# Gathers by row list in a sparse two-layer graph kernel: indices clamped in the list step, no bound on the gathers

## The chip, the cores and the metric

The kernel runs on one core of one Trainium2 chip. The metric is the device time of one execution in microseconds (us); the number given for the kernel before is the median of three runs. Beside these runs, one execution was recorded by the hardware profiler, and every duration of a single instruction below comes from that record.

## The reference

The inputs are 3327 nodes with 512 features each (`x`), and one weighted adjacency matrix `adj` (3327 x 3327, float32). An edge exists with a probability that falls with both node numbers, so the first nodes (hubs) have many neighbours and the last ones few; every node has an edge to itself. Two layers follow each other; each normalizes first and adds its result to `x`:

```python
# layer 0
h = relu(layernorm(x))
x = x + adj @ (relu(adj @ (h @ W1) + b1) @ W2) + b2
# layer 1
h = relu(layernorm(x))
ts = adj @ h
attn_a = sigmoid(concat([ts, h]) @ Wa.T + ba)      # attn_b: same with Wb, bb
g = h @ W_sa
scores = (g @ a_left)[:, None] + (g @ a_right)[None, :]
e = where(adj != 0, exp(-leaky_relu(scores, 0.01)), 0)
x_a = (e / (sum(e, axis=1) + 1e-5)) @ g
x_b = adj @ (h @ W_gcnb) + b_gcnb
x = x + sigmoid(attn_a * x_a + attn_b * x_b)
```

Layer 0 is done with dense products over the whole matrix. Layer 1 needs, for a group of nodes, only the rows of `h` for which the matrix isn't zero, and the kernel uses that.

## The kernel before

The nodes are padded to 3328 (`NP`), 26 blocks (`NB`) of 128. The matrix comes in transposed and padded with zeros (`adjT`), so row 3327, the last one, holds only zeros. A row of `adjT` is also seen as 104 groups (`NG`) of 32 floats (`GW`), 128 bytes each: `adj_groups` lists them all, row by row.

**Pass 1** makes the first product of layer 0. It goes over 7 chunks of 512 columns (the last has 256) and in each over 26 row blocks `j`. SyncE loads a 128 x 512 tile `a` of the matrix into one of 8 buffers; TensorE adds it to `acc_u` (line 512); VectorE takes the largest absolute value of every group of 32 columns into `most` (line 516). Both readers have to be done before the buffer is loaded again.

From `most` the generator `make_lists` makes, a chunk later, the lists for layer 1: for each block of 128 nodes, which is 4 groups of 32, the numbers of the rows that have a nonzero in the group. It is moved forward one step behind each `most` of the next chunk, so its small VectorE operations (`at` L446, `past` L463, `jb` L468 and L469, then `row_h` L473 and `row_a` L476) and its small matmuls (`p_list` L457) lie among the large ones. A batch handles up to 18 list columns of 128 places; 16 batches make 228 columns (`NL`). `rooms` says how many places per group a block has: 9, 8, 7, 6 and 6 for blocks 1 to 5, then 5, 4 and in the end 3, each times 64. Block 0, the hubs, is treated densely (`acc_hub`, line 644).

The number of a list place is computed in float32 in `jb`. A place that no row fills, an empty place, gets a number of at least 3328. Two int32 lists are written from `jb`: `row_h`, the row number with 3327 as its maximum, and `row_a`, row number times 104 plus the group's number, the index of a 128-byte group.

**Pass 2** makes the second product of layer 0 (`acc_g`, line 685) with the matrix loaded again, then the new rows `x` and `h`. The rows of `h`, 520 floats long with a node's score in column 512, are stored to `h_rows` in memory.

**Gathers.** Both lists are used by one helper, `gather` (line 139), which issues an indirect DMA from GpSimd (POOL) for one list column: 128 indices, one row for each partition. 228 of them fetch adjacency groups into `ae` during passes 1 and 2. They are issued in the order of `gather_adj`, each behind one matmul of line 512 or 685 (`gather_behind`, which skips every third or fifth). The `ae` tiles are set to zero at the start (line 379). The other 228 fetch rows of `h` in stage 3 into a cycle of 16 pairs of buffers, shown as `rows` and `hr`.

**Stage 3** is layer 1, block by block from 25 down to 1. `attend` issues a block's row gathers, adds the scores (L800), takes the exponential and masks it by the gathered adjacency (`masked_exp`, L206 to L208); `sums` multiplies weights by rows (`acc`, L829); `turn` transposes (`ptt`, L843), `weigh` multiplies by `W_gcnb` and `W_sa` (`p_b` L883, `p_a` L890), `finish` writes the result. The order in which the engines get this is written out by hand with `queued` (after these instructions), and `pace` holds the gathers of a block behind the sums of the block three or four before (`LEAD`).

A gather here carries the bound that the change is about: with `bounds_check=last, oob_is_err=False` an index above `last` is skipped, and the destination keeps what it held. The bound is an operand in a register. In `row_a` the empty places exceed it; in `row_h` none do.

Of the kernel before, what the change touches and what calls it, by code (L numbers as in the profile page):

```python
# [11 lines left out]
ALU = mybir.AluOpType  # L12
# [34 lines left out]
def kernel(  # L47
# [17 lines left out]
    nc = tc.nc  # L65
    NP, D = x.shape
# [5 lines left out]
    NG = NP // GW  # L72
# [39 lines left out]
    h_dram = dram.tile([NP, ROW], F32, tag="h_rows", name="h_rows")  # L112

    row_h = kept([P, NL], "row_h", I32)
    row_a = kept([P, NL], "row_a", I32)
# [5 lines left out]
    def segments(i):  # L121
# [9 lines left out]
    rows = [  # L131
        hubp.tile([P, 2, ROW], F32, tag=f"rows{k}", name=f"rows{k}", bufs=1) for k in range(NR // 2)
    ]
# [1 line left out]
    for t in rows:  # L135
        nc.vector.memset(t[:, :, D:], 0.0)

    def gather(dst, table, rows, last):
        return nc.gpsimd.indirect_dma_start(  # L139
            out=dst, out_offset=None, in_=table,  # L140
            in_offset=bass.IndirectOffsetOnAxis(ap=rows, axis=0),
            bounds_check=last, oob_is_err=False,
        )

    adj_groups = adjT.rearrange("j (b i) -> (j b) i", i=GW)
# [2 lines left out]
    def gather_adj():  # L148

        for i in range(1, NB):  # L150
            r = rooms[i]
            for k0, k1 in segments(i):
                for q in range(2):
                    for k in range(k0, k1):
                        while (i, q) not in listed:
                            yield None
                        f = first[i] + q * r + k
                        yield gather(
                            ae[i][:, 2 * k0 + q * (k1 - k0) + k - k0, :GW], adj_groups,
                            row_a[:, f : f + 1], NP * NG - 1,  # L160
                        )

    columns = gather_adj()
# [52 lines left out]
    with (  # L216
# [165 lines left out]
        def make_lists(c, most):  # L382


            c0, w = chunks[c]
            g0, n = c0 // GW, w // GW

            def small(shape, name, dtype, bufs=2):
                return l0w.tile(shape, dtype, tag=name, name=f"{name}_{c}", bufs=bufs)

            flag = small([P, MG, NB], "flag", BF16)
            nc.vector.tensor_scalar(flag[:, :n, :], most[:, :n, :], 0.0, None, op0=ALU.is_gt)

            upto = small([P, MG, NB], "upto", BF16)
            flat = "p b j -> p (b j)"
            nc.vector.tensor_tensor_scan(
                upto[:, :n, :].rearrange(flat), begin[:, :n, :].rearrange(flat),
                flag[:, :n, :].rearrange(flat), 0.0, op0=ALU.mult, op1=ALU.add,
            )
            count = small([P, MG], "count", BF16)  # L400
            nc.vector.tensor_copy(count[:, :n], upto[:, :n, NB - 1])
            after = small([P, MG, NB], "after", BF16)
            nc.vector.tensor_tensor(
                after[:, :n, :], count[:, :n].unsqueeze(2).to_broadcast([P, n, NB]),
                upto[:, :n, :], ALU.subtract,
            )
            yield
            p_off = bank(psB, f"p_off_{c}")
            nc.tensor.matmul(p_off[:, :n], before, count[:, :n], start=True, stop=True)
            nc.tensor.matmul(p_off[:, MG : MG + n], every, count[:, :n], start=True, stop=True)  # L410
            offset = small([P, MG], "offset", F32)
            nc.vector.tensor_copy(offset[:, :n], p_off[:, :n])
            nc.vector.tensor_tensor(
                size[:, g0 : g0 + n], p_off[:, MG : MG + n], limit[:, g0 : g0 + n], ALU.is_gt
            )


            step = steps[c % 2]
            p_sh = bank(psB, f"p_sh_{c}")
            nc.tensor.matmul(  # L420
                p_sh[:, : n * NB], shift, after[:, :n, :].rearrange(flat), start=True, stop=True
            )
            nc.vector.tensor_tensor(
                step[:, :n, :NB], p_sh[:, : n * NB].rearrange("p (b j) -> p b j", j=NB),
                upto[:, :n, :], ALU.add,
            )
            yield
            batches = []
            for i in range(c0 // P, (c0 + w) // P):
                for q in range(2 if rooms[i] else 0):  # L430
                    if not batches or sum(rooms[k] for k, _ in batches[-1]) + rooms[i] > CW // NT:
                        batches.append([])
                    batches[-1].append((i, q))
            for batch in batches:
                col = {}
                m = 0
                for i, q in batch:
                    col[i, q] = m
                    m += rooms[i]
                f0 = first[batch[0][0]] + batch[0][1] * rooms[batch[0][0]]  # L440
                at = l0w.tile([P, CW // NT, 2, HALF], BF16, tag="at", name=f"at_{f0}")
                for i, q in batch:
                    r, k = rooms[i], col[i, q]
                    for h in range(2):
                        b = NQ * i + 2 * h + q - g0
                        nc.vector.tensor_scalar(  # L446
                            at[:, k : k + r, h, :],
                            place_row[:, : r * HALF].rearrange("p (k m) -> p k m", m=HALF),
                            offset[:, b : b + 1], None, op0=ALU.is_ge,
                        )  # L450
                    yield
                pl = bank(psB, f"p_list_{f0}")
                plv = pl[:, : m * NT].rearrange("p (c j) -> p c j", j=NT)
                for i, q in batch:
                    for k in range(col[i, q], col[i, q] + rooms[i]):
                        for h in range(2):
                            nc.tensor.matmul(  # L457
                                plv[h * HALF : (h + 1) * HALF, k, :], at[:, k, h, :],
                                step[:, NQ * i + 2 * h + q - g0, :], start=True, stop=True,
                            )  # L460
                yield
                past = l0w.tile([P, CW // NT, NB], BF16, tag="past", name=f"past_{f0}", bufs=1)
                nc.vector.tensor_tensor(  # L463
                    past[:, :m, :], plv[:, :, :NB],
                    place_col[:, f0 : f0 + m].unsqueeze(2).to_broadcast([P, m, NB]), ALU.is_le,
                )
                jb = l0w.tile([P, CW // NT], F32, tag="jb", name=f"jb_{f0}")
                nc.vector.tensor_reduce(jb[:, :m], past[:, :m, :], axis=AX.X, op=ALU.add)  # L468
                nc.vector.scalar_tensor_tensor(  # L469
                    jb[:, :m], jb[:, :m], float(P), plv[:, :, NB], op0=ALU.mult, op1=ALU.add  # L470
                )

                nc.vector.tensor_scalar(  # L473
                    row_h[:, f0 : f0 + m], jb[:, :m], float(NP - 1), None, op0=ALU.min
                )
                nc.vector.scalar_tensor_tensor(  # L476
                    row_a[:, f0 : f0 + m], jb[:, :m], float(NG), group_col[:, f0 : f0 + m],
                    op0=ALU.mult, op1=ALU.add,
                )
                listed.update(batch)  # L480
                yield
# [285 lines left out]
    with tc.tile_pool(name="spw", bufs=2) as spw:  # L767
# [8 lines left out]
        def attend(i, seg):  # L776
# [11 lines left out]
            hr = taken[i][k0] = []  # L788
            for k in range(n):
                hr.append(next(pairs))  # L790
                for q in range(2):
                    f = first[i] + q * r + k0 + k
                    with queued(gathered[0]):
                        gathered[0] = gather(
                            hr[k][:, q, :], h_dram[:, :], row_h[:, f : f + 1], NP - 1
                        )
                    lead = LEAD[i < NB - 8]
                    if k0 + k + q == 0 and len(combined) >= lead:
                        pace(gathered[0], combined[-lead])
                nc.vector.tensor_tensor(  # L800
                    e.rearrange("p (q k) i -> p k q i", q=2)[:, k],
                    s_l, hr[k][:, :, D : D + 1].to_broadcast([P, 2, GW]), ALU.add,
                )
# [3 lines left out]
            if k0:  # L807
                part = spw.tile([P, 2, GW], F32, tag="part", name=f"part_{i}_{k0}")
            last = nc.vector.tensor_reduce(
                part, e.rearrange("p (q k) i -> p q i k", q=2), axis=AX.X, op=ALU.add  # L810
            )
            if k0:
                last = nc.vector.tensor_tensor(es, es, part, ALU.add)
# [121 lines left out]
        ty, last = copy_out(NB - 1, taken[NB - 1]["acc"])  # L935
        turning = NB - 1, ty, taken[NB - 1]["es"]
        held = [copied, last]
        for i in range(NB - 2, 1, -1):
# [18 lines left out]
            ty, last = copy_out(i, taken[i]["acc"])  # L957
# [159 lines left out]
```

## Time and profile before

| | |
|---|---|
| median of three runs | 844.46 us (844.13 to 846.61) |
| span of the profiled execution (first to last instruction) | 840.2 us |
| median less span | 4.3 us |
| TensorE busy | 781.6 us, 93% of the span |
| VectorE busy | 515.6 us, 61% |
| GpSimd busy | 493.4 us, 59% |
| mean granted TensorE clock | 0.973 of full speed |
| bytes moved by DMA | 200.14 MB |
| list step (first `jb` to last `row_a`) | 73.3 to 245.6 us |
| adjacency gathers | 76.3 to 423.5 us |
| row gathers | 444.8 to 792.0 us |

For the profiled execution only the span is recorded; its own total isn't listed, so the median stands beside it. The busy share of an engine is a mean over stages that differ: pass 1 ends near 210 us, pass 2 near 440 us, and stage 3 takes the rest. In the rows that follow, the number after the bar is the busy time of a group, then the mean ns of one instruction, and after the second bar the idle time just before them with what ended most of it. "issue" means that the engine waited for nothing that the profile shows.

### The profile page before, as it was taken

To read this page: it belongs to the slowest core of one execution; us is meant where nothing else is said; L and a number is where in the kernel's file an instruction comes from. 1 tells how busy PE (TensorE), PEld (TensorE's weight loads), DVE (VectorE), ACT (ScalarE), POOL (GpSimd) and SP (SyncE) were. 2 spreads that over 40 slices of the span, in tenths; PEclk is the share of its full clock that TensorE was granted. 3 is DMA by queue.
4 is the path that set the end of the run, shared out by engine and by line. 5 is a ranking of instruction groups with operands and counts; after the bars stand their busy time and mean duration, and the time that the engine had idled before them with its cause. 6 is when DMAs were issued, how large, how long until landed. Compare 5 with 4: busy or idle time off the path is not lost.

```text
span 840.2 us, 12143 instructions
## 1 busy us (share of the span) xinstructions
PE 781.6 (93%) x3615; PEld 416.9 (50%) x3615; DVE 515.6 (61%) x1658; ACT 187.6 (22%) x396; POOL 493.4 (59%) x513
## 2 busy tenths in 40 slices
PE   9999899999799999999999599799998999999795
PEld 7774344445443444444464366455554555454363
DVE  7778989999646866685775455345535353443342
ACT  7770000000002313033052022122222222121121
POOL 3202756676677777776716555666766767667400
PEclk9999999999799999999999799899999999999798
DMA  8787998898578989998958556787788867777600
GB/s 272 242 292 227 330 283 262 285 299 276 151 236 297 368 281 306 319 343 284 345 180 260 158 182 196 216 227 217 225 225 215 228 203 227 207 210 209 187 26 30
DMA packets 106891, 200.14 MB, mean 238 GB/s; under 512 B 16801, under 2 KB 30656, under 8 KB 106816
## 3 DMA queue, kind: packets, MB, share of 16 engines
q1 hardware_dynamic: 72592, 124.40, 45.2%
q0 software_dynamic: 25536, 63.74, 27.9%
q10 hardware_dynamic: 8688, 11.15, 3.8%
q8 instruction: 30, 0.49, 0.2%
q14 instruction: 45, 0.37, 0.1%
HBM read 179.39 MB, written 20.55 MB: 238 GB/s over the span
## 4 chain that ended last, share of the span: by engine, by line
PE 66%; issue 18%; DMA 7%; DVE 5%; another core or an unknown queue 3%; ACT 1%; SPq 0%; ACTq 0%; DVEq 0%
PE acc L829 14%; PE p_b L883 12%; PE p_a L890 11%; PE acc_g L685 10%; PE acc_u L512 5%; PE acc_hub L644 3%; DMA a<-in_adjT_dram 3%; PE ptt L843 3%; PE pu L291 3%; PE px L587 2%; DMA W_sa_sb<-in_W_sa_dram 1%; PE pt L283 1%; DMA xb<-in_x_dram 1%; DVE junk L563 1%
## 5 line engine op out<-in xcount | busy, mean ns | idle before, releaser
L139 POOL DMA_INDIRECT ae<-in_adjT_dram,row_a x228 | 246.4, 1081 | 151.6 <-issue 57.8
L139 POOL DMA_INDIRECT hr<-h_rows,row_h x140 | 144.1, 1029 | 64.5 <-issue 30.8
L685 PE MATMUL acc_g<-a,g 128*128 128x512 f32 (+1 forms) x364 | 160.3, 575 | 5.7 <-DMA a<-in_adjT_dram 3.8
L512 PE MATMUL acc_u<-a,rows 128*128 128x512 f32 (+1 forms) x364 | 159.9, 578 | 2.8 <-DMA a<-in_adjT_dram 2.2
L139 POOL DMA_INDIRECT rows<-h_rows,row_h x88 | 90.7, 1031 | 69.2 <-DVE e_hub L206 20.3
L883 PE MATMUL p_b<-W_g_sb,tyT 128*128 128x257 f32 x416 | 102.0, 395 | 16.3 <-issue 15.7
L516 DVE TENSOR_REDUCE most<-a 128x16 f32<-128x512 f32 (+1 forms) x182 | 110.6, 638 | 6.1 <-DMA a<-in_adjT_dram 5.2
L685 PEld LDWEIGHTS acc_g<-a,g 128*128 128x128 f32 x364 | 67.0, 192 | 85.5 <-issue 61.1
L883 PEld LDWEIGHTS p_b<-W_g_sb,tyT 128*128 128x128 f32 x416 | 78.3, 193 | 48.5 <-issue 19.3
L890 PE MATMUL p_a<-W_sa_sb,tyT 128*128 128x512 f32 (+2 forms) x216 | 97.5, 590 | 3.5 <-issue 3.1
L512 PEld LDWEIGHTS acc_u<-a,rows 128*128 128x128 f32 x364 | 66.5, 194 | 58.7 <-issue 51.9
L829 PE MATMUL acc<-hr,ae 64*64 64x512 f32 x560 | 81.7, 612 | 3.2 <-issue 2.3
L858 DVE COPY tyT<-ptt 128x512 f32<-128x512 f32 x51 | 34.9, 686 | 54.2 <-PE acc L829 21.8
L890 PEld LDWEIGHTS p_a<-W_sa_sb,tyT 128*128 128x128 f32 x216 | 41.1, 193 | 47.1 <-issue 45.6
L208 DVE SCALAR_TENSOR_TENSOR ae<-ae 128x192 f32<-128x192 f32 (+2 forms) x36 | 12.5, 368 | 79.1 <-issue 29.9
L829 PE MATMUL acc<-rows,ae 64*64 64x512 f32 x352 | 49.0, 607 | 1.7 <-issue 1.4
L829 PEld LDWEIGHTS acc<-hr,ae 64*64 64x64 f32 x560 | 30.9, 137 | 39.2 <-issue 37.9
L748 ACT ACTIVATE f<-f 128x2 f32<-128x2 f32 x26 | 5.3, 203 | 166.9 <-DVE f L747 118.4
L300 ACT ACTIVATE gT<-acc_u,b_col 128x512 f32<-128x512 f32 (+1 forms) x7 | 4.6, 657 | 157.1 <-issue 101.3
L563 DVE SCALAR_TENSOR_TENSOR junk<-rows,w_rows 128x512 bf16<-128x512 f32 x52 | 35.7, 686 | 3.0 <-issue 0.5
L716 DVE TENSOR_TENSOR xb<-xb,b_row 128x512 f32<-128x512 f32 x26 | 17.7, 689 | 30.4 <-DMA xb<-in_x_dram 19.6
L843 PEld LDWEIGHTS ptt<-ident,ty 128*128 128x128 f32 x208 | 24.5, 144 | 19.1 <-issue 18.2
(142 smaller groups left out, 907.5 us busy)
## 6 DMA issues: line engine op xcount, KB each, us to landing
a<-in_adjT_dram SPq DMA_DIRECT2D x338, 256.0 KB
h_rows<-rows SPq DMA_DIRECT2D x26, 260.0 KB
x<-in_x_dram SPq DMA_DIRECT2D x26, 256.0 KB
xb<-in_x_dram SPq DMA_DIRECT2D x26, 256.0 KB
x<-xb ACTq DMA_DIRECT2D x26, 256.0 KB
x1b<-x SPq DMA_DIRECT2D x26, 256.0 KB
out_dram<-va SPq DMA_DIRECT2D x25, 256.0 KB
ae<-in_adjT_dram,row_a POOLq DMA_INDIRECT x228
```

The lines of the kernel that those rows point to most:

```text
L139: return nc.gpsimd.indirect_dma_start(out=dst, out_offset=None, in_=table, in_offset=bass.IndirectOffsetOnAxis(ap=rows, axis=0), bounds_ch ...
L291: nc.tensor.matmul(pu[:, :HID], hT[:, k, :], W1_sb[:, k, :], start=(k == 0), stop=(k == KD - 1))
L512: added = nc.tensor.matmul(acc[:, :w], u[j], a[:, :w], start=(j == 0), stop=(j == NB - 1))
L516: nc.vector.tensor_reduce(most[:, : w // GW, j], a[:, :w].rearrange("p (b i) -> p b i", i=GW), axis=AX.X, op=ALU.max, apply_absolute_value ...
L563: return nc.vector.scalar_tensor_tensor(junk, h, 1.0, w_rows[:, s, :], op0=ALU.mult, op1=ALU.mult, accum_out=into)
L644: nc.tensor.matmul(acc_hub[k], s, hrow[i % NR][:, :D], start=(i == 0), stop=(i == NB - 1))
L685: added = nc.tensor.matmul(acc[:, :w], g[j], a[:, j % per, :], start=(j == 0), stop=(j == NB - 1))
L829: added = nc.tensor.matmul(taken[i]["acc"][h][q * HALF : (q + 1) * HALF, :], both[half_p, q * n + k, :], taken[i][k0][k][half_p, q, :D], s ...
L843: moved = nc.tensor.transpose(pt[:, k * P : (k + 1) * P], ty[h][:, k * P : (k + 1) * P], ident)
L858: last = nc.vector.tensor_copy(dst, src)
L883: nc.tensor.matmul(p_b[n][:, :WH], tyT[:, k, 0, :], W_g_sb[:, k, n * WH : (n + 1) * WH], start=(k == 0), stop=(k == KD - 1),)
L890: last = nc.tensor.matmul(p_a[:, c0:c1], tyT[:, k, 1, :], W_sa_sb[:, k, c0:c1], start=(k == 0), stop=(k == KD - 1),)
```

## The change

The helper no longer sets a bound. In the list step the minimum of `jb` and 3327 is written back into `jb`, a copy converts it into `row_h`, and `row_a` is computed from the clamped `jb`. The real list places get the same indices as before. An empty place now has the index of its group in the last row, and its gather fetches 128 bytes of zeros where before it was skipped.

```diff
-    def gather(dst, table, rows, last):
+    def gather(dst, table, rows):
         return nc.gpsimd.indirect_dma_start(
             out=dst, out_offset=None, in_=table,
             in_offset=bass.IndirectOffsetOnAxis(ap=rows, axis=0),
-            bounds_check=last, oob_is_err=False,
         )
...
                         yield gather(
                             ae[i][:, 2 * k0 + q * (k1 - k0) + k - k0, :GW], adj_groups,
-                            row_a[:, f : f + 1], NP * NG - 1,
+                            row_a[:, f : f + 1],
                         )
...
-                nc.vector.tensor_scalar(
-                    row_h[:, f0 : f0 + m], jb[:, :m], float(NP - 1), None, op0=ALU.min
-                )
+                nc.vector.tensor_scalar(jb[:, :m], jb[:, :m], float(NP - 1), None, op0=ALU.min)
+                nc.vector.tensor_copy(row_h[:, f0 : f0 + m], jb[:, :m])
                 nc.vector.scalar_tensor_tensor(
                     row_a[:, f0 : f0 + m], jb[:, :m], float(NG), group_col[:, f0 : f0 + m],
                     op0=ALU.mult, op1=ALU.add,
                 )
...
                         gathered[0] = gather(
-                            hr[k][:, q, :], h_dram[:, :], row_h[:, f : f + 1], NP - 1
+                            hr[k][:, q, :], h_dram[:, :], row_h[:, f : f + 1]
                         )
```

In the built program 456 register moves on POOL, one ahead of each gather, are gone; VectorE has 16 more operations, one copy for each batch. The order of POOL's and ScalarE's instructions is the same. On TensorE some 27 instructions around `acc_u`, `p_list` and the turns of pass 1 stand a few places earlier or later, and so do some of `at` and `most` on VectorE.

## The prediction

> **What bounds the kernel now.** I begin with the page's first part, busy time by engine, and its fifth, the costliest groups, of which I take the three gather rows.
>
> ```profile
> PE 781.6 (93%) x3615; PEld 416.9 (50%) x3615; DVE 515.6 (61%) x1658; ACT 187.6 (22%) x396; POOL 493.4 (59%) x513
> ...
> q0 software_dynamic: 25536, 63.74, 27.9%
> ...
> L139 POOL DMA_INDIRECT ae<-in_adjT_dram,row_a x228 | 246.4, 1081 | 151.6 <-issue 57.8
> L139 POOL DMA_INDIRECT hr<-h_rows,row_h x140 | 144.1, 1029 | 64.5 <-issue 30.8
> ...
> L139 POOL DMA_INDIRECT rows<-h_rows,row_h x88 | 90.7, 1031 | 69.2 <-DVE e_hub L206 20.3
> ```
>
> TensorE is 93% busy, so over the whole kernel nothing else can gain much. GpSimd is 59% busy, nearly all of it 228 + 228 gathers. The gathers' own queue (q0) takes 27.9% of the DMA engines' time. The shares differ by stage, so I read one window in pass 1, one in pass 2, one in stage 3. Columns: window, us, then busy us of PE, PEld, DVE, ACT, POOL, then PE clock, DMA share, GB/s.
>
> ```profile
> 100.00:200.00 100.00, 95.56 (x480) 43.45 (x478) 94.13 (x242) 2.06 (x3) 63.74 (x63) 0.98 0.90 285
> 300.00:400.00 100.00, 97.26 (x232) 41.79 (x230) 66.63 (x222) 26.40 (x50) 74.21 (x66) 1.00 0.93 310
> 600.00:700.00 100.00, 95.67 (x530) 53.31 (x530) 45.66 (x165) 22.22 (x49) 70.98 (x69) 1.00 0.79 222
> ```
>
> In pass 1 two engines are full, TensorE and VectorE (94%), and the DMA share is 0.90; in pass 2 TensorE and the DMA (0.93); in stage 3 TensorE alone. VectorE in pass 1 is where the new copy goes, the DMA in passes 1 and 2 is where the padded fetches go. Next, who waits in 80 to 210 us (total us, times, longest):
>
> ```profile
> PE acc_u L512 <- DMA a<-in_adjT_dram: 2.2, 1, 2.2
> PE p_list L457 <- DVE at L446: 1.0, 2, 0.5
> PE p_list L457 <- DVE row_a L476: 0.9, 1, 0.9
> ...
> DVE past L463 <- PE acc_u L512: 5.5, 6, 2.5
> DVE most L516 <- DMA a<-in_adjT_dram: 1.5, 2, 0.9
> ```
>
> In 130 us TensorE waits 1.9 us for VectorE (L457, twice for `at`, once for `row_a`), and VectorE 5.5 us for TensorE: they run in step, VectorE slightly ahead. SyncE's loads of adjacency tiles wait 25.9 us there for `acc_u` and 11.3 us for `most` to free a buffer, so VectorE also meters the transfers.
>
> **What the Trainium skill says.** "DMA: Bandwidth & Descriptors", section "SWDGE vs HWDGE vs iDMA": descriptors of a GpSimd DMA are computed in software on the GpSimd's cores. The trace agrees in so far as a gather occupies POOL for 1.00 us whether its rows have 128 or 2080 bytes. The same page, "Issuing engines are not separate DMA queues": DMAs of all issuers share 16 engines and interleave. So extra gather bytes compete with the tiles that SyncE loads; q0 and q1 are each spread over the 16 in the packet records. "VectorE: DVE Perf Modes", section "TRN2 errata — SBUF-src ops pay a fixed extra latency per instruction": a measured fixed term of about 150 cycles at 0.96 GHz, 156 ns. The trace agrees: 160 to 168 ns for the 16-column operations below. No page prices a bound on the indices.
>
> **The change, part by part.** First the bound. The built program loses 456 register moves on POOL, one per gather; its order and waits are otherwise as before.
>
> ```profile
> L139 POOLq MOVE  x456: 29/29/29, 24.0 to 790.4; - x152
> ...
> L139 POOL DMA_INDIRECT ae<-in_adjT_dram,row_a x228: 991/997/2724, 76.3 to 423.5; - x114
> L139 POOL DMA_INDIRECT hr<-h_rows,row_h x140: 992/998/1328, 450.1 to 772.3; - x140
> ```
>
> 456 × 29 ns = 13.2 us of POOL's sequencer. It is work in the 0.30 us between gathers: the timeline has them at 444.77, 446.15, 447.45, 448.75, 450.06, a period of 1.30 us. Where that shows:
>
> ```profile
> 444.77 1.08 POOL L139 DMA_INDIRECT rows<-h_rows,row_h  x1 [20.29 <-DVE e_hub L206]
> ...
> 456.11 0.22 DVE L800 TENSOR_TENSOR ae<-s_left,hr 128x64 f32<-128x64 f32 x1 [1.12 <-DMA hr<-h_rows,row_h]
> ...
> 457.92 1.19 PE L829 MATMUL acc<-rows,ae 64*64 64x512 f32 x8 [0.80 <-issue]
> ```
>
> In passes 1 and 2 POOL waits for the pace (22.5 us for `acc_u`, 11.9 for `acc_g`) and has 20.29 us between its last adjacency gather and the first row gather, so there the saving is hidden. At the start of stage 3 the six gathers of block 25 and their landings lead to the first scores at 456.11 and the first sum at 457.92, before which TensorE idles 0.80 us. Six moves are 6 × 29 = 0.17 us; I take −0.3, since the instruction may also shorten a little, with at most −0.8 (the whole idle time). Late next is the 9.4 us for which TensorE idles from 461.85 (`p_b` L883, "issue"), which may swallow it. Later in stage 3 a block of 3 places takes POOL 6 × 1.30 = 7.8 us of a block's 10.8 us, of 4 places 10.4 of 12.4, of 5 places 13.0 of 14.7; gathers land two to three blocks ahead of use. Those moves hide behind TensorE's sums and weights, and cost nothing if that cover goes, since they are only removed.
>
> What the trace doesn't show is a gather without a bound. In the one direction: the 1.00 us holds for gathers with no empty place and with 60% of them, so the test of an index costs nothing that depends on its outcome; a compare less per descriptor is worth at most a tenth of the instruction (my guess), −0.1 us each. In the other: if descriptors come from another routine, it could be slower; the slack above is the protection. I take 0, and keep ±0.1 us in the range, which gives −0.6 to +0.6 us at the start of stage 3 and nothing beyond, unless the coupling of rival D is real.
>
> Second, the copy. Before, each of 16 batches ended in these three:
>
> ```profile
> L469 DVE SCALAR_TENSOR_TENSOR jb<-jb,p_list x16: 145/160/166, 74.4 to 245.3; 128x16 f32<-128x16 f32 x5, 128x18 f32<-128x18 f32 x3, 128x14 f32<-128x14 f32 x2, 128x15 f32<-128x15 f32 x2
> L473 DVE TENSOR_SCALAR row_h<-jb x16: 155/166/361, 75.1 to 245.5; 128x16 int32<-128x16 f32 x5, 128x18 int32<-128x18 f32 x3, 128x14 int32<-128x14 f32 x2, 128x15 int32<-128x15 f32 x2
> L476 DVE SCALAR_TENSOR_TENSOR row_a<-jb,group_col x16: 154/168/293, 75.2 to 245.6; 128x16 int32<-128x16 f32 x5, 128x18 int32<-128x18 f32 x3, 128x14 int32<-128x14 f32 x2, 128x15 int32<-128x15 f32 x2
> ```
>
> Now the minimum goes back into `jb` and a copy follows it: 16 × 0.16 = 2.6 us more on VectorE. Behind it on VectorE are `row_a` and the next reductions `most`; for `row_a` wait the batch's gathers (hidden: nothing reads them before stage 3), for `most` the next loads, and for `at` the `p_list` matmuls. Both ends: 0, if VectorE's 5.5 us of waits for TensorE absorb it; +2.6, if all of it pushes through `most` to the tiles. The waits say VectorE is mostly ahead, the 94% says not by much. I choose a third, +0.9. The scheduler also moves some 27 matmuls of `acc_u` and `p_list` by a few places; nothing is added there, ±0.4.
>
> Third, the padded places. Of 29,184 list places 5,888 (20.2%) are empty; in the packet records their `ae` descriptors are 4 bytes long. Now each fetches 128 zero bytes from the last row: 0.75 MB of 200. Full packets of 8 groups have a median of 46 ns, packets of 528 bytes 28, of 32 bytes 13; filling them adds 24.9 us of engine time, 1.6 us for each of the 16 engines, spread over 350 us in which they are busy 0.90 to 0.93. Many of these fetches meet in one row of 13 KB. Row gathers already do this: wholly empty ones have packets of 327 ns on average, those without an empty place 229, a factor of 1.43. If packets with padding were to take 0.6 us each, it would be 308 engine-us, 19 us per engine, of which the idle tenth (some 30 us) takes most. TensorE waits for tiles only 2.2 us in pass 1 and 3.8 in pass 2. I take a third of 1.6, +0.5; from 0 to +4. Row gathers are unchanged, since they clamped before.
>
> Sum: −0.3 + 0.9 + 0 + 0.5 = **+1.1 us**. The profiled execution spans 840.2 us, the median of three runs is 844.46, so 4.3 us lie outside the span and stay. 844.5 + 1.1 = **845.6**. About 0.3%, 2.5 us, is what a measurement of this kernel can tell from no change.
>
> **Rivals.**
> *B, VectorE and the hot row push through (slower).* If each added VectorE operation delays the loads by its length, +2.6, and padded fetches delay tiles by 2 to 4 us more, the total is +4 to +6: **849 to 850**. It decides once more than 2.5 us are exposed. For it: VectorE at 94%, DMA at 0.90. Against it: few waits name either one.
> *C, the gather gets slower (slower).* In stage 3, 348 us hold 228 × 1.30 = 296 us of gathers. From 1.55 to 1.60 us a period POOL becomes the bound, with 23 us for each further 0.1 us; at 1.65 it is about **856**. Against it: fewer operands, no known extra work.
> *D, the gather gets shorter and stage 3 answers (faster).* In blocks of 5 or more places TensorE has gaps of 0.7 and 1.35 us that no wait explains, 18 us in all, often in step with landings of gathers. If periods of 1.15 us remove a quarter of them and the start gains 0.8: −5.3 + 1.4 = −4, **840.5**. Against it: a gap in step with a landing need not come from it.
> *E, nothing shows*: the bound cost no visible time, and all is hidden: **844.5**, within my likeliest case.
>
> **How the numbers follow.** Likeliest case with E 0.50, B 0.26, C 0.07, D 0.17. The likeliest case's own range is 843.5 to 847.5, of which a tenth passes 847.0: faster 0.17, same 0.45, slower 0.38. The range to hold 8 in 10 takes in most of B and D and leaves out C: 840.5 to 850.5.
>
> **What would show it.** Right: DMA_INDIRECT stays at about 1.00 us, no MOVE on L139, the period 1.27 to 1.30 us, VectorE in 100:200 about 1.4 us busier, every `ae` packet of 1024 bytes, q0 up by 0.75 MB. For B, `acc_u` waits for `a` tiles grow by over 2 us; for C or D the gather's median leaves 1.00 by over 0.1 us and the time of stage 3 moves with it. I am wrong if stage 3's length, 457.92 us to the end, changes by over 2 us while gathers keep their length.

## The result, and the profile after

The changed kernel takes 853.74 us (median of four runs, 853.16 to 855.52) against 844.3 us (842.81 to 846.61) for the kernel before on the same chip. The ratio is 1.0111, with a 95% interval of 1.0072 to 1.015: 9.4 us slower, where the forecast was 845.6 us with a range of 840.5 to 850.5.

The profiled execution of the changed kernel spans 853.8 us, 13.6 more than that of before. It is the longest of the four runs (855.52 us), so the two traces differ by more than the medians do; and only 1.7 us of it lie outside the span, where the forecast had carried 4.3. First the page of the changed kernel, busy time by engine, the gathers' queue and the gather groups:

```profile
PE 783.4 (92%) x3615; PEld 416.9 (49%) x3615; DVE 517.4 (61%) x1674; ACT 187.1 (22%) x396; POOL 463.1 (54%) x513
...
q0 software_dynamic: 25536, 64.47, 28.3%
...
L139 POOL DMA_INDIRECT ae<-in_adjT_dram,row_a x228 | 229.0, 1004 | 178.0 <-issue 67.4
L139 POOL DMA_INDIRECT hr<-h_rows,row_h x140 | 136.5, 975 | 75.1 <-issue 31.7
```

TensorE does 1.8 us more in a span that is 13.6 us longer: the loss is idle time. GpSimd is busy 30 us less. The same windows as before show where (window, us, busy us of PE, PEld, DVE, ACT, POOL, clock, DMA share, GB/s):

```profile
100.00:200.00 100.00, 95.93 (x497) 42.82 (x497) 93.00 (x249) 2.06 (x3) 58.62 (x62) 0.98 0.92 282
300.00:400.00 100.00, 93.68 (x225) 40.86 (x224) 64.22 (x215) 23.62 (x46) 65.74 (x64) 1.00 0.92 300
600.00:700.00 100.00, 96.52 (x528) 54.67 (x526) 45.54 (x158) 21.96 (x48) 64.67 (x68) 1.00 0.76 221
```

In pass 2 TensorE falls from 97.26 to 93.68 us of 100 and the DMA from 310 to 300 GB/s; stage 3 is as full as it was. Of the 3.6 us in pass 2, 2.7 are a single wait of TensorE at 308.0 that no transfer ends ("issue"). Set side by side, `acc_g`, with which pass 2 begins, starts 4.9 us later than before (225.04 against 220.19, and not near 210), it ends 11.2 us later, and the first sum of stage 3 comes 12.0 us later (469.95 against 457.92). From there to the end it is 383.9 us against 382.3. So 12.0 of the 13.6 us lie ahead of stage 3. What each line of the list step and of the gathers does now, from the views of the tile `jb` and of line 139:

```profile
L472 DVE TENSOR_SCALAR jb<-jb x16: 156/165/409, 74.9 to 251.3; 128x16 f32<-128x16 f32 x5, 128x18 f32<-128x18 f32 x3, 128x14 f32<-128x14 f32 x2, 128x15 f32<-128x15 f32 x2
L473 DVE CAST row_h<-jb x16: 159/168/402, 75.6 to 251.5; 128x16 int32<-128x16 f32 x5, 128x18 int32<-128x18 f32 x3, 128x14 int32<-128x14 f32 x2, 128x15 int32<-128x15 f32 x2
...
L139 POOL DMA_INDIRECT ae<-in_adjT_dram,row_a x228: 938/944/2717, 76.8 to 434.2; - x114
L139 POOL DMA_INDIRECT hr<-h_rows,row_h x140: 940/946/1340, 461.9 to 788.2; - x140
```

The copy is the CAST of 168 ns. A gather is 53 ns shorter, 944 instead of 997, and no MOVE is left on line 139. TensorE's waits from 80 to 245 us name no transfer that is worse than before, where the wait for tiles was 2.2 us in pass 1:

```profile
PE pw L549 <- DVE junk_w L545: 4.3, 1, 4.3
PE p_list L456 <- DVE at L445: 3.2, 1, 3.2
PE acc_u L510 <- DMA a<-in_adjT_dram: 2.3, 2, 1.7
PE pg L302 <- ACT gT L299: 1.8, 1, 1.8
```

Yet the second long wait, for `at`, begins with TensorE itself. The timeline around it:

```profile
213.07 2.42 PE L510 MATMUL acc_u<-a,rows 128*128 128x256 f32 x10
...
216.85 0.65 DVE L462 TENSOR_TENSOR past<-p_list,place_col 128x468 bf16<-128x468 f32 x1 [4.04 <-PE acc_u L510]
216.95 0.94 POOL L139 DMA_INDIRECT ae<-in_adjT_dram,row_a  x1 [1.63 <-PE acc_u L510]
...
218.65 0.20 PE L456 MATMUL p_list<-step,at 128*64 128x27 bf16 x1 [3.15 <-DVE at L445]
```

TensorE's recorded work ends at 215.49. VectorE and GpSimd both wait for TensorE, and both go on within 0.1 us of each other, 1.4 us after that end. TensorE then waits for what VectorE had not been able to make. The records don't say what held TensorE's results back. In pass 2, too, more of the added wait is of this unnamed kind than for tiles. Before:

```profile
PE acc_g L685 <- DMA a<-in_adjT_dram: 3.8, 7, 1.1
...
PE acc_g L685 <- issue: 1.9, 6, 0.8
```

And after:

```profile
PE acc_g L683 <- issue: 5.3, 5, 2.7
PE acc_g L683 <- DMA a<-in_adjT_dram: 4.8, 7, 1.2
```

### The profile page after: what moved, and what is told of

The parts are those of the page before. It is cut to its first block, busy times and chain, and to the rows that moved or that the text cites. A ratio compares the mean times of both kernels' runs of the same rounds, so it can differ in the third digit from the quotient of the medians.

```text
span 853.8 us, 11703 instructions
## 1 busy us (share of the span) xinstructions
PE 783.4 (92%) x3615; PEld 416.9 (49%) x3615; DVE 517.4 (61%) x1674; ACT 187.1 (22%) x396; POOL 463.1 (54%) x513
## 5 line engine op out<-in xcount | busy, mean ns | idle before, releaser
L139 POOL DMA_INDIRECT ae<-in_adjT_dram,row_a x228 | 229.0, 1004 | 178.0 <-issue 67.4
L139 POOL DMA_INDIRECT hr<-h_rows,row_h x140 | 136.5, 975 | 75.1 <-issue 31.7
L683 PE MATMUL acc_g<-a,g 128*128 128x512 f32 (+1 forms) x364 | 159.7, 573 | 10.2 <-issue 5.3
L510 PE MATMUL acc_u<-a,rows 128*128 128x512 f32 (+1 forms) x364 | 161.9, 579 | 3.3 <-DMA a<-in_adjT_dram 2.3
L139 POOL DMA_INDIRECT rows<-h_rows,row_h x88 | 85.5, 971 | 75.8 <-ACT e_hub L206 21.6
L881 PE MATMUL p_b<-W_g_sb,tyT 128*128 128x257 f32 x416 | 104.4, 395 | 21.6 <-issue 11.5
L881 PEld LDWEIGHTS p_b<-W_g_sb,tyT 128*128 128x128 f32 x416 | 77.6, 193 | 56.1 <-issue 17.9
L827 PE MATMUL acc<-hr,ae 64*64 64x512 f32 x560 | 79.5, 618 | 3.2 <-issue 1.7
L753 DVE TENSOR_TENSOR vb<-p_b,bg_row 128x257 f32<-128x257 f32 x26 | 11.0, 424 | 40.4 <-remote 14.9
```

Of the source, the lines that this page charges most:

```text
L139: return nc.gpsimd.indirect_dma_start(out=dst, out_offset=None, in_=table, in_offset=bass.IndirectOffsetOnAxis(ap=rows, axis=0),)
L510: added = nc.tensor.matmul(acc[:, :w], u[j], a[:, :w], start=(j == 0), stop=(j == NB - 1))
L683: added = nc.tensor.matmul(acc[:, :w], g[j], a[:, j % per, :], start=(j == 0), stop=(j == NB - 1))
L827: added = nc.tensor.matmul(taken[i]["acc"][h][q * HALF : (q + 1) * HALF, :], both[half_p, q * n + k, :], taken[i][k0][k][half_p, q, :D], s ...
L881: nc.tensor.matmul(p_b[n][:, :WH], tyT[:, k, 0, :], W_g_sb[:, k, n * WH : (n + 1) * WH], start=(k == 0), stop=(k == KD - 1),)
```

## The experiments

Three theories. **Theory 1**: the copy on VectorE, and the order of matmuls that comes with it. **Theory 2**: the fetches of padded places. **Theory 3**: the gather without a bound itself. The kernel before took 764 us on three of the chips that ran these (called 764 chips below) and 842.5 us on a fourth (the 842 chip), which resembles the one of the first comparison. Every ratio is to the kernel before on the same chip. It comes with its 95% interval and isn't simply the quotient of two medians; the two can differ by a few thousandths.

### One part at a time, on a 764 chip

These four were expected in times of a kernel of 844 us. On this chip it takes 764 us, and in none of the four does the loss of 5 us and more show that they forecast for theories 1 and 2; so they can only divide a smaller one.

The list step of the change, with the bound kept:

> The list step of the change (clamp in place, copy, all indices in range) with the bound left on every gather; the order on every engine is that of the changed kernel. Theory 1, the copy and the order that comes with it: 850 to 855 us, with pass 1 and the first chunk of pass 2 about 7 us longer than before. Theory 2, the fetches of padded places: 850 to 855 us, the loss spread over pass 2. Theory 3, the gather without a bound itself: back at 843 to 846 us. In all cases a gather takes 1.00 us, not 0.94.

Measured: 767.25 against 763.57 us, ratio 1.0037 (1.002 to 1.0055).

```profile
L139 POOLq MOVE  x456: 29/29/29, 24.9 to 726.0; - x152
...
L139 POOL DMA_INDIRECT ae<-in_adjT_dram,row_a x228: 991/997/2716, 77.0 to 407.7; - x114
```

The gather has its 997 ns and its moves back, so the 53 ns belong to the bound. The list step, with the fetches that follow from it, costs 2.8 us here (the change in ratio times 764).

No bound and no copy:

```diff
-                nc.vector.tensor_scalar(jb[:, :m], jb[:, :m], float(NP - 1), None, op0=ALU.min)
-                nc.vector.tensor_copy(row_h[:, f0 : f0 + m], jb[:, :m])
+                nc.vector.tensor_scalar(
+                    row_h[:, f0 : f0 + m], jb[:, :m], float(NP - 1), None, op0=ALU.min
+                )
                 nc.vector.scalar_tensor_tensor(
-                    row_a[:, f0 : f0 + m], jb[:, :m], float(NG), group_col[:, f0 : f0 + m],
+                    row_a[:, f0 : f0 + m], row_h[:, f0 : f0 + m], float(NG), group_col[:, f0 : f0 + m],
```

> No bound on any gather and padded places fetched, but row_a is computed from the clamped int32 row_h, so that there is no copy and TensorE's order is that of the kernel before. Theory 1 (copy and order): 843 to 846 us. Theory 2 (padded fetches): 849 to 854 us, with pass 2 longer by 4 us or more. Theory 3 (no bound): 849 to 854 us. A gather takes 0.94 us.

Measured: ratio 1.0015 (0.9995 to 1.0035), not clear of no change.

The copy alone (to the kernel before; `jc` is a temporary):

```diff
+                nc.vector.tensor_scalar(jc[:, :m], jb[:, :m], float(NP - 1), None, op0=ALU.min)
+                nc.vector.tensor_copy(row_h[:, f0 : f0 + m], jc[:, :m])
```

> Only the copy and the order that comes with it: the minimum goes into a temporary, a copy makes row_h, row_a is computed from the unclamped number, and the bound stays, so empty places are skipped as before. Theory 1: 849 to 854 us. Theories 2 and 3: 844 to 846 us (16 copies of 0.16 us, at most 2.6 us).

Measured: ratio 1.0015 (0.9998 to 1.0032), 1.1 us. Theory 1 alone can't carry the 2.8 us of the list step.

The bound off the row gathers only (to the kernel before, `last` is None there):

```diff
-            bounds_check=last, oob_is_err=False,
+            **({} if last is None else dict(bounds_check=last, oob_is_err=False)),
...
-                            hr[k][:, q, :], h_dram[:, :], row_h[:, f : f + 1], NP - 1
+                            hr[k][:, q, :], h_dram[:, :], row_h[:, f : f + 1], None
```

> The kernel before with the bound dropped from the 228 row gathers alone; list step, order and adjacency gathers as before. If a gather of 0.94 us instead of 1.00 disturbs stage 3 (theory 3), stage 3 gets 2 us or more longer: 846 to 848 us. If it helps the start and the steps of stage 3: 841 to 843.5 us. If it is hidden: 844 us.

Measured: 762.87 us, ratio 0.9977 (0.9961 to 0.9993). On this chip this version is faster than the kernel before, by 1.8 us by the ratio and by 0.7 us by the medians. Of theory 3 the opposite is true here: a shorter gather helps a little.

### The whole change again, and the fetches by themselves

> The changed kernel unaltered, beside the other three on one chip. If parts add up as ratios to the kernel before: the list step with the bound kept gave 1.0037 and dropping the bound from the row gathers 0.9977, so about 1.001 to 1.002. If the loss belongs to the change wherever it runs: 1.008 to 1.014, as in the first comparison.

Measured: ratio 1.0014 (0.9995 to 1.0033), another 764 chip. Here the change costs 1.1 us, and the parts add up: list step +0.37%, row gathers −0.23%. They do so without any share for the bound on the adjacency gathers, which the first part keeps and the changed kernel hasn't.

The padded fetches alone: the diff of "no bound and no copy", with the bound kept.

> The bound stays on every gather, row_a is computed from the clamped int32 row_h, so there is no copy and TensorE's order is that of the kernel before; the one difference in the work is that 5,888 empty places are fetched. Theory 2 (padded fetches): 1.002 to 1.004, the share of the list step with bound (1.0037) that the copy alone (1.0015) leaves, or more. Theory 1 (copy and order): 0.999 to 1.001.

Measured: ratio 1.0042 (1.0026 to 1.0059). With VectorE's work and TensorE's order as before, the fetches alone cost as much as the whole list step. On the 764 chips theory 2 holds.

All places skipped (to the kernel before):

```diff
-                            row_a[:, f : f + 1], NP * NG - 1,
+                            row_a[:, f : f + 1], 0,
```

> The kernel before with the bound of the adjacency gathers set to 0, so that all 29,184 places are skipped and no adjacency group is fetched (layer 1 then has zero weights); order and list step as before. It gives the price of the 23,296 groups fetched before, and a quarter of it is what 5,888 more would cost. Theory 2: 2 to 8 us faster than before. Theories 1 and 3: within 1.5 us of it.

Measured: ratio 0.9957 (0.9935 to 0.9978), 3.3 us faster. So 23,296 ordinary fetches cost 3.3 us (1.7 to 5.0) and 5,888 padded ones 3.2 (2.0 to 4.5).

Padded places over 128 rows (no bound, no copy; `tail` is filled by an iota with 3327 minus the partition's number; some 20 instructions of TensorE stand elsewhere):

```diff
-                    row_h[:, f0 : f0 + m], jb[:, :m], float(NP - 1), None, op0=ALU.min
+                    row_h[:, f0 : f0 + m], jb[:, :m], tail[:, 0:1], None, op0=ALU.min
```

> No bound, no copy; row numbers are limited to 3327 minus the partition's number instead of 3327, so the empty places of a gather fall on 128 rows (real rows above the limit move too, which changes some sums). Against the same without spread (1.0015): if the padded row is a hot spot, 0.997 to 0.999, and row packets of wholly empty gathers in stage 3 take about 229 ns on average and not 327. If not: 1.001 to 1.003.

Measured: ratio 1.0012 (0.9995 to 1.0028), not to be told from 1.0015 without the spread. The row packets did what the expectation of a hot spot says: those of wholly empty gathers in stage 3 take 223 ns on average here (218 and 233 in the two repeats below) and 302 to 366 in the profiles in which they meet in one row; gathers without an empty place take 219 to 230 in all. So the one row is a hot spot for the packets, and on the 764 chips the kernel's time doesn't show it.

### The same on the 842 chip

> The changed kernel once more, with the three below on one chip. On a chip where the kernel before takes about 764 us: 1.001 to 1.002 of it. On a chip where it takes about 844 us, as in the first comparison: 1.008 to 1.014 if the loss belongs to that chip, 1.001 to 1.002 if the first comparison was a chance.

Measured: ratio 1.0118 (1.0071 to 1.0165). The loss of the first comparison was no chance, and its size belongs to the chip.

> No bound, padded places fetched, no copy, TensorE's order as before. At about 764 us: 1.001 to 1.002. At about 844 us: 1.008 or more if the fetches (theory 2) make the loss of the first comparison, under 1.002 if the copy and its order (theory 1) do.

Measured: ratio 1.0079 (1.0053 to 1.0104).

> The copy and its order, the bound off the row gathers only, empty places skipped. At about 764 us: the sum of the two parts, 1.0015 and 0.9977, so 0.999. At about 844 us: 1.006 or more if theory 1 makes the loss, under 1.000 if theory 2 does.

Measured: ratio 1.0022 (1.0002 to 1.0043).

> The bound off the row gathers only, all else as before: 0.997 to 0.999 on either chip, and so a version that beats both kernels. The gain lies at the end of stage 3, where blocks have six places and more: from the first sum of block 4 to the last of block 1 about 0.9 us shorter than with the bound.

Measured: ratio 1.0012 (0.9988 to 1.0036). No gain there, against the expectation.

Both kernels that fetch padded places lose 0.8 to 1.2%, both that skip them 0.1 to 0.2%. Between the second and the fourth, 5.6 us apart by their ratios (0.67% of 842.5), the copy plays no part: what differs is the fetches, and with them the bound on the adjacency gathers. The first and the third differ in the same two things, here by 8.1 us. The two weren't taken apart on this chip. On the 764 chips the bound on the adjacency gathers made no difference that can be measured.

### What remained open

Was it the number of the fetches, the one row, or the bound on the adjacency gathers? For the 842 chip this stays open: the following runs, which bear on it, are all of 764 chips.

> Bound kept, padded places fetched, no copy. At about 844 us: 1.006 or more if the fetches themselves make the loss, under 1.002 if it needs adjacency gathers without a bound. At about 764 us: 1.002 to 1.006, as before.

Measured: ratio 1.0031 (1.0012 to 1.005).

> No bound, no copy, empty places spread over 128 rows (the row limit is 3327 minus the partition's number, which moves some real rows too). At about 844 us: under 1.003 if the one padded row is a hot spot, 1.006 or more if the number of fetches counts and not their place. At about 764 us: 1.001 to 1.003.

Measured: ratio 1.0013 (0.9992 to 1.0035).

> All 29,184 adjacency places are skipped (layer 1 has zero weights). If every fetch costs the same, it is faster than before by four times what the 5,888 padded ones cost: at about 844 us 0.97 to 0.975, at about 764 us 0.985 to 0.99 (0.9957 was measured there). If the padded ones are dear because they meet in one row: 0.993 to 0.998 on either.

Measured: ratio 0.995 (0.993 to 0.9971): 3.8 us for the ordinary fetches, 2.4 us for the padded ones in the same comparison. By the values of the two comparisons a padded place costs two to four times an ordinary one; in this one the intervals leave room for equal cost, in the first they don't. The result is the one forecast for padded places that are dear because they meet in one row; as spreading them over 128 rows gains no time, it doesn't prove that reason.

> The changed kernel as it is, as the measure for the three above on the same chip: 1.009 to 1.014 at about 844 us, 1.000 to 1.003 at about 764 us.

Measured: ratio 1.0012 (0.9995 to 1.003).

> As padded_rows_spread. In the packet records there, an adjacency gather with 120 or more empty places took 1.1 to 1.4 us of engine time (1.5 to 1.75 with all in one row). At about 844 us: 1.003 to 1.005 if the one row makes half of the loss (engine time of such a gather falls from 2.3 us to about 1.2), 1.007 or more if it makes none. At about 764 us: 1.001 to 1.002.

Measured: ratio 1.0023 (1.0006 to 1.0041).

> As padded_fetch_alone: the bound kept, padded places fetched in one row, no copy. At about 844 us: 1.006 to 1.010, with 6 to 7 us more engine time for each of the 16 DMA engines. At about 764 us: 1.003 to 1.004 with 3 to 3.5 us.

Measured: ratio 1.0058 (1.0033 to 1.0082).

The packet records of the gathers' queue say more than the times. Each adjacency gather has 16 data packets. The table has the time that they took on the DMA engines in one profiled execution: the sum of all 228 gathers in us, then the mean of the 150 gathers that have no empty place, and of the 22 with 120 to 128 of them. The packets are given to the gathers in order of their start, 16 at a time; neighbours can mix, so these means are approximate, and the sums are not.

| kernel, chip | sum | no empty place | 120 and more |
|---|---|---|---|
| before, first comparison | 223 | 1.14 | 0.29 |
| changed, first comparison | 326 | 1.28 | 2.04 |
| row gathers without bound, 842 | 224 | 1.16 | 0.29 |
| copy, and row gathers without bound, 842 | 255 | 1.33 | 0.29 |
| no copy, no bound, 842 | 332 | 1.24 | 2.27 |
| changed, 842 (an execution of 860.8 us) | 313 | 1.24 | 1.99 |
| row gathers without bound, 764 | 246 | 1.32 | 0.38 |
| copy alone, 764 | 241 | 1.28 | 0.35 |
| no copy, no bound, 764 | 297 | 1.21 | 1.71 |
| list step with bound, 764 | 317 | 1.27 | 1.51 |
| changed, 764 (two) | 298, 288 | 1.24, 1.17 | 1.49, 1.47 |
| padded fetch alone, 764 (three) | 300, 290, 289 | 1.21, 1.13, 1.17 | 1.67, 1.75, 1.69 |
| padded rows spread, 764 (three) | 293, 279, 298 | 1.24, 1.28, 1.31 | 1.41, 1.08, 1.34 |
| nothing fetched, 764 (two) | 50, 50 | 0.22, 0.22 | 0.22, 0.22 |

A gather that meets in the last row costs the engines 1.2 to 1.55 times an ordinary one on the 764 chips and 1.6 to 1.8 times where the kernel takes 842 us and more. With the rows spread it is 0.8 to 1.1. This is the hot spot again.

Over all gathers the fetches add 103 us of engine time in the first comparison and 107 between the two kernels without the copy on the 842 chip, 6.4 and 6.7 us for each of the 16 engines; the losses there are 9.4 and 5.6 us. Between the two kernels with the copy, 8.1 us apart, it is 58 us, 3.6 for each engine. On the 764 chips it is mostly about 50 (45 to 73 in seven profiles), 3.1 us each, for losses of 2.4 to 4.4 us. So loss and added time of an engine are of one size, but they don't agree pair by pair. Whether spreading would save time on the 842 chip isn't settled: it wasn't run there. On the 764 chips it saves none that can be measured.

## Why the prediction was wrong

**The padded places** are the step that failed: the term of +0.5 us, with 0 to +4 as its bounds. It is a product of two factors, and both were too small.

The first is the added engine time. The prediction took it from medians (46, 28 and 13 ns) and got 24.9 us; measured, it is 103 us. With the mean of a full packet in the kernel before, 73 ns, the same filling comes to 42 us. The other 61 us is that the packets themselves became longer: 89 ns on average in the changed kernel, with a tenth of them at 189 ns and more. On the 764 chips the mean is enough: the two kernels there that skip only empty places have means of 80 and 82 ns, which gives 50 and 53 us, and about 50 came. The prediction had the hot row in view, but put the term at the median. Its ceiling of 308 engine-us also counts only the 513 packets that are wholly empty; 965 packets have padding, so its 0.6 us each would make 579. The hot row itself is a small part of what came: 22 gathers at 2.04 instead of 1.28 us are 17 us of the 103, by an estimate from the table.

The second factor is how much of it shows. A third was taken, on the ground that TensorE seldom waits for a tile and the idle tenth takes the rest. On the 764 chips the padded fetches alone show about whole: 3.1 us more for each DMA engine, 3.3 us more time as the mean of three comparisons. On the slower chips 5.6 to 8.1 us lie between kernels with and without them, beyond the bound of +4, though there the bound on the adjacency gathers is gone too. That the ordinary fetches hide better (194 us of engine time between "nothing fetched" and the two that skip only empty places, 12 us for each engine, for 3.3 and 3.8 us) is measured as well; why is open.

How the engine time reaches TensorE isn't shown either. Ahead of the first sum of stage 3 TensorE idles 29.3 us in the changed kernel and 19.3 before, but its waits for tiles grow by only 1.1 us, from 2.2 to 2.3 us in pass 1 and from 3.8 to 4.8 in pass 2. The DMA share of 0.93 in pass 2 was the warning, and "DMA: Bandwidth & Descriptors", section "Issuing engines are not separate DMA queues", of the Trainium skill names the sharing. The trace of before agrees in so far as packets of loads are in flight during 95% of the time in which there are packets of gathers (80 to 430 us). But the loads' packets of 2048 bytes hardly lengthen with the fetches, from 98.2 to 98.9 ns on average in pass 2.

**The copy** was sized well. +0.9 us was taken; the copy alone gave 1.1 us on a 764 chip, and on the 842 chip 0.8 us lie between the two kernels that skip, one with and one without it. Neither value is clear of no change. VectorE is busy 1.8 us more over the span; in the window from 100 to 200, where 1.4 us more were forecast, it is busy 1.1 us less.

**The bound** was not free of effect: a gather takes 944 ns against 997, where 1.00 us was taken and up to 0.1 us allowed. The 0.30 us between gathers stayed though the moves were gone, so the moves had been hidden there; the period is 1.25 us. The 0.3 us that was to be saved at the start of stage 3 did not come: from the first row gather to the first sum it is 13.15 us before and 13.16 after.

Rival D's mechanism exists, with another place. On the 764 chips the sums from block 23 to block 3 take the same time to 0.01 us in all profiles; but from the first sum of block 3 (not block 4, as the expectation has it) to the last of block 1 it is 44.16 us in each of seven profiles without the bound on row gathers, and 45.00 to 45.35 in seven with it. These blocks have 7 to 9 places, and the prediction had carried its working only to blocks of five: 14 gathers of 1.25 us are 17.5 us, while the step from block 3 to block 2 takes 14.25. On the chips at 842 us and more it is 53.5 to 56.1 us in four profiles against 59.2 in the one with it, but from block 23 into block 13 the four are 4 us longer, so nothing is left. Why isn't known.

**Rival B** came nearest: +4 to +6 us. Its sign was right, and of its two parts the fetches and not VectorE's operations; it had 0.26 where the likeliest case had 0.50. **Rival C** is out: the gather got shorter. **Rival E**, that nothing shows, is out on the slower chips; on the 764 chips the whole change can't be told from it.

The remaining difference is the chip. On a 764 chip the change measures 1.0014 and 1.0012, which is +1.1 and +0.9 us: the forecast sum of +1.1, though by other terms (fetches +3.3, copy +1.1, bound −1.8, in sum +2.6; each is uncertain by a microsecond and more). So the agreement there is luck. The forecast was made from the trace of a chip on which the fetches cost up to twice the engine time, and whose TensorE stands idle 48.1 us in the kernel before and 59.6 after, against 9 to 14 us on the others.

## What to carry to other kernels

Price an added transfer by the mean of its packets and not by the median, and count that as the lower end: here it was right on one kind of chip and less than half of what came on the other. Where a stage keeps the DMA over nine tenths busy, take all of it as exposed until a run says otherwise. An index that is skipped was worth keeping here, where a fifth of the list is empty. Where every index is in range (here the row gathers), giving up the bound shortened each gather, and that showed only where the gathers took longer than the work they feed, and on one kind of chip. The same change cost 9 to 10 us on one kind of chip and about 1 us on another, so a small ratio is measured on more than one.

## What had not been expected of the hardware

The same kernel took 764 us on three chips and 842 to 844 us in the two comparisons of the other kind. The kernel with the bound off the row gathers has a profile on both kinds, with spans of 762.4 and 840.2 us. Between its first and last matmul TensorE is idle 9.4 us in the one and 51.5 in the other, so a little over half of the difference is waits. The rest is busy time, 742.7 against 778.3 us. Single instructions are nearly as long (a `p_b` matmul 386 against 398 ns); they follow each other at greater distances: from the first sum of block 13 to that of block 3 it is 124.4 against 147.4 us.

The longest wait comes after the first transposes `ptt`. In the kernel before, first comparison ("remote" is a release that the profile can't name):

```profile
460.75 1.09 PE L843 MATMUL ptt<-ident,ty 128*128 128x128 f32 x8
...
470.38 0.59 ACT L902 COPY ty<-acc 128x512 f32<-128x512 f32 x1 [11.87 <-remote]
470.48 1.29 DVE L858 COPY tyT<-ptt 128x512 f32<-128x512 f32 x2 [9.14 <-remote]
...
471.23 1.23 PE L883 MATMUL p_b<-W_g_sb,tyT 128*128 128x257 f32 x2 [9.38 <-issue]
```

And at the same place with the bound off the row gathers, on a 764 chip:

```profile
442.14 1.09 PE L843 MATMUL ptt<-ident,ty 128*128 128x128 f32 x8
442.18 0.59 ACT L902 COPY ty<-acc 128x512 f32<-128x512 f32 x1 [3.93 <-PE acc L829]
...
442.84 1.29 DVE L858 COPY tyT<-ptt 128x512 f32<-128x512 f32 x2 [1.76 <-PE ptt L843]
443.58 1.79 PE L883 MATMUL p_b<-W_g_sb,tyT 128*128 128x257 f32 x7 [0.35 <-DVE tyT L858]
```

In the first, ScalarE's wait for the sums and VectorE's for the transposes both end at 470.4, 8.6 us after TensorE's recorded work; in the second VectorE begins 0.7 us after the transposes do. The changed kernel has the same wait of 9.35 us at the same place, and the smaller one at 215.5 us is of the same kind. The prediction took this wait and the smaller gaps of stage 3 for gaps of the program ("issue"), and priced rival D by the smaller ones; on the 764 chips TensorE idles at most 2.5 us from the first sum on.

The granted clock differs as well. Its rows, in tenths of full speed over 40 slices, of the kernel before and of the one with the bound off the row gathers on a 764 chip:

```profile
PEclk9999999999799999999999799899999999999798
```

```profile
PEclk9999999999999999999999999999999999999998
```

The record behind the rows has the clock at half in short stretches. Without the last one, behind the last sums, they make 37.5 to 41.0 us in the three kernels on the slower chips that skip the empty places, 47.8 to 61.4 us in the three that fetch them, and 0 to 10.2 us on the 764 chips. In the kernel before, a stretch of 10.2 us begins 4.6 us after the start of the longest wait. Whether the waits bring the low clock or both have one cause, no run here shows. What holds TensorE's results back, and whether the padded fetches lengthen it, stays open.
